# When VectorE makes its sums: gates moved to the turning of tokens, and the second layer's sums of weights made in two parts, in a mixture-of-experts kernel on one Trainium2 core

## The chip, the cores and the metric

The kernel runs on one core of a Trainium2 chip. Its time is the device time of one execution in microseconds (us); less is better. The engines appear in the profile under short names: PE is TensorE (matrix products; PEld is its loading of weights), DVE is VectorE, ACT is ScalarE, POOL is GpSimd, and SP is SyncE, whose queue issues most DMAs. Each engine works through its own queue in order and waits at an instruction until the semaphores that it names have been raised. A "bank" is one of the accumulators in PSUM that TensorE writes and the other engines read.

## What is computed

For 4096 tokens of 256 numbers, in float32:

```python
# graph layer
f = layernorm(x)
h = adj @ (f @ neigh_W.T) / (adj.sum(1) + 1)
x = x + concat([f, h]) @ lin_W.T
# attention (4 heads, 2 kv heads, causal), then a mixture of experts, on layernorm(x)
z = layernorm(x)
z = z + attention(rmsnorm(z)) @ wo.T
flat = rmsnorm(z)
weights = top 2 of softmax(flat @ router_w.T), made to add up to 1      # 8 experts
out = 0
for e in range(8):
    hh = silu(flat @ w1[e].T) * (flat @ w3[e].T)                        # 682 wide
    out = out + weights[:, e] * (hh @ w2[e].T)
x = x + z + out
```

The change touches the last loop alone. The number `weights[:, e]` of a token is called its gate here.

## The kernel before

The program has three stages: the graph layer to about 530 us, attention to about 1044 us, and the experts from there to the end. Tokens are not multiplied with all 8 experts. During attention each block of tokens is routed, and the row of a token (its 256 numbers, its number, its 8 gates) is scattered by GpSimd into the lists of its two experts in DRAM. The expert stage then works on groups: whole groups of 256 rows of one expert, and smaller ones of 128 rows for the ends of the lists. There are 42 turns, k = 0 to 41; `TURNS[k]` is the group of a turn. From k=9 whole and small groups alternate, with two small ones in a row at times.

Nothing is reordered by a scheduler: the order of each engine's queue is the order in which the functions below are called. The main loop calls, for each turn k: `hidden(k)` or `hidden_seven(k)` (first layer), then `combine(k - 1)` (second layer of the turn before, and scattering into the result), and then, if the group of turn k-1 was a whole one, `sums13` for a later turn. Loads of rows and weights are issued by SP four to five turns ahead.

What each function puts into the queues:

- `prepare(k)` (L1373) turns the rows of turn k on TensorE (L1379, tile `tx`) and ScalarE copies them, scaled, to SBUF (L1385, `xT`). For some turns it also makes sums of them on VectorE (`sums_x`, L1439). It is called for turn k+1 inside the first layer of turn k.
- `hidden(k)` multiplies in the plain way: products into banks `h` (L1656), ScalarE's silu (L1662), VectorE's multiply into `hT` (L1663, L1675). It takes six banks of the pool `e_h` in rotation, two at a time.
- `hidden_seven(k)` (L1445) does the first layer of a whole group with seven products in place of eight (a Strassen-Winograd scheme). It is used in 13 turns: k = 12, 14, 17, 19, 21, 23, 26, 28, 30, 33, 35, 37 and 39. The 682 columns are split into a part `one` of four chunks and a part `two` of one chunk; each has three banks, A, D and B, of the same six. Bank A takes several products one after another, and between them it has to be read: ScalarE copies it (L1490), VectorE adds it to a tile in SBUF (L1493). The tiles are `wqkv_sb` or `qT_all` (sums with banks B and D) and `hy` for part `one`, `hz` for part `two`. Four steps matter in what follows: `added_up` adds banks B and D, `third` adds bank A into `hy` or `hz`, `last` puts one more product into bank A, which must wait for that, and `multiplied` (L1521 to L1525) makes the hidden numbers, its second multiply (L1523) being the last reader of bank A. The first products of the next turn go into bank A of part `one`.
- `split(k)` (L1560) makes four sums of the hidden numbers on VectorE (L1571 to L1574), and `sums2(k)` four sums of the second layer's weights, called T1, T3, T2 and T4 in that order (L1589 to L1592), each 128x384. Both are inputs of `seven_products(k)` (L1595), the second layer of a whole group, which runs one turn later. In the 13 turns `hidden_seven` calls `sums2` before its first products; in the other turns with `seven_products` (k = 4 to 8 and 10) `split` calls it.
- `sums13` (L1410) makes four sums of a later turn's first-layer weights on GpSimd (L1422 to L1425), each 128x640.
- `combine(k)` (L1684) first computes the gates: VectorE multiplies the 8 gates of each row with a one-hot row of the group's expert (`pick`, L1691) and adds them up (`gt`, L1695). Then come the products of the second layer (L1613, or L1717 for small groups) into banks `ye_y` and `ye_ms`, seven VectorE adds for a whole group (L1621 to L1627), the multiplication with the gate (L1728 on ScalarE, L1734 on VectorE) and one or two scatters by GpSimd (L1739), which add the rows into DRAM. A scatter waits until that of the group before has landed.

The order of VectorE's work in `hidden_seven` is set by its last lines, of which these matter:

```python
            sums2(k)
            begun(one)
            second(one)
            added_up(one)
            step()
            begun(two)
            third(one)
            second(two)
            ...
            added_up(two)
            gated(one)
            third(two)
            step()
            if behind is not None:
                prepare(behind, p_ms, "ms")
            ...
            last(one)
            last(two)
            multiplied(one)
```

Of the kernel before, what the change touches and what calls it, by code (L numbers as in the profile page):

```python
# [9 lines left out]
F32 = mybir.dt.float32  # L10
# [3 lines left out]
ALU = mybir.AluOpType  # L14
AX = mybir.AxisListType
PSUM = bass.MemoryType.PSUM

P = 128
N = 4096
C = 256  # L20
# [4 lines left out]
NE = 8  # L25
# [36 lines left out]
ROW = C + 1 + NE  # L62
# [3 lines left out]
def fast_kernel(  # L66
# [24 lines left out]
    nc = tc.nc  # L91
# [89 lines left out]
    vv = [kvp.tile([P, TB, NKV * HD], F32, name=f"vv{b}") for b in range(NB)]  # L181
# [58 lines left out]
    with (  # L240
# [117 lines left out]
        G11, G12, G21, G22, T1, T2, T4 = range(7)  # L358
        T3 = G12
# [303 lines left out]
    with (  # L663
# [566 lines left out]
        mine = eg.tile([P, NG, NE], F32, name="mine")  # L1230
# [105 lines left out]
            at2 += (pt_all[:, at + 2 * W13 : at + 2 * W13 + W2],)  # L1336
        w13s = [a.rearrange("p (c w) -> p c w", c=2) for a in at13]
        w2s = [a.rearrange("p (k c) -> p k c", k=NF + 1) for a in at2]
        rows, hidden_of, inputs_of, expert_of = {}, {}, {}, {}


        def halves(i):
# [30 lines left out]
        def prepare(k, pool=p_y, tag="y"):  # L1373
            i = TURNS[k]
            n = halves(i)
            tr = pool.tile([P, 2, n, P], F32, tag=tag, name=f"tx_{i}")
            for h in range(n):
                for c in range(2):
                    nc.tensor.transpose(  # L1379
                        tr[:, c, h, :], rows[i][:, h, c * P : (c + 1) * P], ident  # L1380
                    )
            xT = late[:, LATE_XT + k % 2 * 2 * GR : LATE_XT + k % 2 * 2 * GR + 2 * n * P]
            xT = xT.rearrange("p (c i) -> p c i", c=2)
            for c in range(2):
                nc.scalar.activation(  # L1385
                    xT[:, c, :], tr[:, c].rearrange("p h i -> p (h i)"), AF.Copy,
                    scale=ln2_sb[:, c : c + 1],
                )
            inputs_of[i] = xT
            if k in SPLIT13:  # L1390
                sums_x(k, tr)

# [4 lines left out]
        parts_of, sums13_of = {}, {}  # L1399
# [28 lines left out]
        def sums_x(k, tr):  # L1428

            xT = inputs_of[TURNS[k]]  # L1430
            room = kT[6 + SPLIT13.index(k) % 2].rearrange("p (n i) -> p n i", n=4)
            m = {f"T{n + 1}": room[:, n] for n in range(4)}
            for c in range(2):
                for h in range(2):
                    m[f"B{c + 1}{h + 1}"] = xT[:, c, h * P : (h + 1) * P]
            for dst, c, h, less in (
                ("T1", 0, 1, "B11"), ("T2", 1, 1, "T1"), ("T3", 1, 1, "B12"), ("T4", 1, 0, "T2"),
            ):
                nc.vector.scalar_tensor_tensor(  # L1439
                    m[dst], tr[:, c, h, :], ln2_sb[:, c : c + 1], m[less],  # L1440
                    op0=ALU.mult, op1=ALU.subtract,
                )
            sums13_of[k].update(m)

        def hidden_seven(k, step, behind):  # L1445

            i = TURNS[k]
            m, xT, w13_sb = sums13_of.pop(k), inputs_of.pop(i), w13s[k % 5]
# [58 lines left out]
            def added_up(q):  # L1507
                added(q.s1, q, q.B)
                added(q.u2, q, q.D)

            def third(q):
                product(q, q.A, "S3", "T3")
                added(q.s5, q, q.A)
# [7 lines left out]
            def multiplied(q):  # L1521
# [2 lines left out]
                    hT[:, q.rows, 0:P], q.s1, q.A[:, 0 : len(q.chunks), :]  # L1524
                )  # L1525

            sums2(k)
            begun(one)
            second(one)
            added_up(one)  # L1530
            step()
            begun(two)
            third(one)
# [7 lines left out]
            added_up(two)  # L1541
            gated(one)
            third(two)
            step()
            if behind is not None:
                prepare(behind, p_ms, "ms")
# [13 lines left out]
        def split(k, hT):  # L1560


            m = {}
            for c in range(2):
                chunks = hT.rearrange("p (j c) i -> p c j i", c=2)[:, c]
                for h in range(2):
                    m[f"A{h + 1}{c + 1}"] = chunks[:, :, h * P : (h + 1) * P]
            for n, s in enumerate(("S1", "S2", "S4")):
                m[s] = kT[k % 2 * 3 + n][:, 0 : 3 * P].rearrange("p (j i) -> p j i", j=3)
            m["S3"] = m["A21"]  # L1570
            nc.vector.tensor_add(m["S1"], m["A21"], m["A22"])  # L1571
            nc.vector.tensor_sub(m["S2"], m["S1"], m["A11"])
            nc.vector.tensor_sub(m["S4"], m["A12"], m["S2"])
            nc.vector.tensor_sub(m["S3"], m["A11"], m["A21"])  # L1574
            if k not in parts_of:
                sums2(k)
            parts_of[k].update(m)

        def sums2(k):

            m = {}
            for c in range(2):
                weights = w2s[k % 5].rearrange("p (j c) o -> p c j o", c=2)[:, c]
                for h in range(2):
                    m[f"G{c + 1}{h + 1}"] = weights[:, :, h * P : (h + 1) * P]
            for n, s in enumerate(("T1", "T2", "T4")):
                m[s] = vv[k % 2 * 3 + n][:, 0:3, :]
            m["T3"] = m["G12"]
            nc.vector.tensor_sub(m["T1"], m["G12"], m["G11"])  # L1589
            nc.vector.tensor_sub(m["T3"], m["G22"], m["G12"])  # L1590
            nc.vector.tensor_sub(m["T2"], m["G22"], m["T1"])
            nc.vector.tensor_sub(m["T4"], m["T2"], m["G21"])  # L1592
            parts_of[k] = m

        def seven_products(k):  # L1595

# [87 lines left out]
        def combine(k):  # L1684
            i = TURNS[k]
            n = halves(i)
            w2_sb = w2s[k % 5]
            hT = hidden_of.pop(i)
            r = rows.pop(i)
            pick = ex.tile([P, n, NE], F32, tag="pick", name=f"pick_{i}")  # L1690
            nc.vector.tensor_mul(  # L1691
                pick, r[:, 0:n, C + 1 : ROW], mine[:, i : i + 1, :].to_broadcast([P, n, NE])
            )
            gt = ex.tile([P, n, 1], F32, tag="gt", name=f"gt_{i}")
            nc.vector.tensor_reduce(gt, pick, AX.X, ALU.add)  # L1695
            if k < ALONE or k % 2:
                y = ax.tile([P, HALF, C], F32, tag="yT1", name=f"y_{i}")
            else:
                y = (
                    pt_all[:, 2 * (2 * W13 + W2) :] if k % 4  # L1700
                    else wo_sb.rearrange("p j o -> p (j o)")[:, 0:512]
                ).rearrange("p (h c) -> p h c", h=HALF)

            last = k >= NM - 2
            seven = k in SEVEN
            if seven:
                done = seven_products(k)
            else:
                ps = [
                    pool.tile([P, HALF, C], F32, tag=tag, name=f"ye_{i}_{tag}")  # L1710
                    for pool, tag in ((p_ms, "ms"), (p_y, "y"))[0 if last else 1 :]
                ]

            def products(h):
                cols = slice(h * P, (h + 1) * P)
                for q in range(NF + 1):
                    nc.tensor.matmul(  # L1717
                        ps[h if last else 0][:, h, :],
                        hT[:, q, cols], w2_sb[:, q, :], start=(q == 0), stop=(q == NF),
                    )  # L1720

            for h in range(0 if last or seven else n):
                products(h)
            for h in range(n):
                if last:
                    products(h)
                if seven or n == 1:
                    nc.scalar.activation(  # L1728
                        y[:, h, :],
                        done[h].rearrange("p h o -> p (h o)") if seven else ps[0][:, h, :],  # L1730
                        AF.Copy, scale=gt[:, h],
                    )
                else:
                    nc.vector.tensor_scalar(  # L1734
                        y[:, h, :], ps[h if last else 0][:, h, :], gt[:, h], None, op0=ALU.mult
                    )
                at = bass.IndirectOffsetOnAxis(ap=r[:, h, C : C + 1].bitcast(I32), axis=0)
                nc.gpsimd.memset(gap, 0.0)  # L1738
                put = nc.gpsimd.indirect_dma_start(  # L1739
                    out=(acc_dram if k < NM - LAST else out)[:, :],  # L1740
                    out_offset=at,
                    in_=y[:, h, :], in_offset=None, compute_op=ALU.add,
                )
                if h:
                    free(put, f"half {i}", "an expert has a token once")
                else:
                    join(put, f"half {i}")
                if i < NA:
                    free(put, "last x", "the tokens of the first groups are others")
                    join(put, "first sums")  # L1750
# [86 lines left out]
        def step():  # L1837
            for f in next(rest, []):
                f()
# [776 lines left out]
```

## Time and profile before

| | us |
|---|---|
| median of 3 runs | 1550.57 |
| lowest and highest run | 1549.93, 1553.36 |
| profiled execution | 1554.68 |
| its span, first to last instruction | 1552.9 |
| TensorE busy in the span | 1533.3 |
| TensorE busy, 1044 to 1535 us (491 us of the expert stage) | 487.6 |
| VectorE busy, 1044 to 1535 us | 322.9 |
| GpSimd busy, 1044 to 1535 us | 208.0 |

The profile is one execution, taken by the hardware profiler. Lines of a timeline give the start in us from the span's start, the duration, the engine, the line of the kernel, the operation, and "out<-in" by the names of tiles, with partitions times elements and the count; in brackets stands how long the engine was idle before it, and what ended that. Groups of one line give minimum, median and maximum in ns. A list of waits gives who waited for whom, with the total, the number of waits and the longest. TensorE's matrix products are pipelined and their ends are modelled: the row of one can overlap the next by some 0.2 us. The granted clock of TensorE is 0.998 over the span.

### The profile page before, as it was taken

What the parts mean: (1) busy time and instruction counts of PE and PEld (TensorE: products, weight loads), DVE (VectorE), ACT (ScalarE), POOL (GpSimd) and SP (SyncE); (2) the same over time, 40 slices, a digit from 0 to 9 for tenths busy, and PEclk for the clock granted to TensorE, in tenths of its full rate; (3) what the DMA queues carried; (4) which work ended last, traced back from release to release, by engine and by line L of the source; (5) the groups of instructions that cost most, each with busy time, mean ns of one, the idle gap of its engine ahead of it and who ended that gap; (6) DMA issues with size and microseconds to landing.
All of it is one profiled execution on the core that took longest, in us unless ns stands there. A gap on an engine that the chain in (4) does not pass through costs nothing. (4 is left out here: it accounts for less than half of the span.)

```text
span 1552.9 us, 28593 instructions
## 1 busy us (share of the span) xinstructions
PE 1533.3 (99%) x11082; PEld 1138.0 (73%) x11082; DVE 1124.1 (72%) x2263; ACT 517.5 (33%) x966; POOL 741.4 (48%) x777
## 2 busy tenths in 40 slices
PE   8999999999999999999999999999999999999997
PEld 7888888888888643444444444358899999999996
DVE  7966677766766677778879878785565667677772
ACT  1101010010010255555656555553122433333331
POOL 3446456565565423364564563442424545545342
PEclk9999999999999999999999999999999999999999
DMA  6434444443434100001010111048676778777855
GB/s 237 129 128 147 139 139 136 139 139 136 139 136 139 35 1 16 29 31 52 32 57 23 39 39 33 25 149 320 205 229 212 223 235 257 243 231 253 264 144 133
DMA packets 68513, 209.42 MB, mean 135 GB/s; under 512 B 17488, under 2 KB 45520, under 8 KB 54736
## 3 DMA queue, kind: packets, MB, share of 16 engines
q1 hardware_dynamic: 55104, 189.50, 35.5%
q0 software_dynamic: 12720, 17.47, 5.7%
q8 instruction: 89, 1.46, 0.4%
q10 hardware_dynamic: 544, 0.52, 0.1%
q14 instruction: 56, 0.46, 0.1%
HBM read 184.48 MB, written 27.13 MB: 136 GB/s over the span
## 5 line engine op out<-in xcount | busy, mean ns | idle before, releaser
L759 PE MATMUL sc<-qT_all,kT 64*64 64x512 f32 (+3 forms) x2304 | 282.0, 557 | 1.0 <-ACT pt_all L767 0.5
L493 PE MATMUL acc<-a,g 128*128 128x256 f32 x1024 | 245.9, 380 | 0.0
L493 PEld LDWEIGHTS acc<-a,g 128*128 128x128 f32 x1024 | 193.0, 190 | 31.5 <-DVE vv L511 1.2
L759 PEld LDWEIGHTS sc<-qT_all,kT 64*64 64x64 f32 x2304 | 91.2, 133 | 130.0 <-issue 108.2
L767 ACT ACTIVATE pt_all<-sc 128x1024 f32<-128x1024 f32 (+3 forms) x157 | 148.9, 955 | 95.8 <-PE sc L759 95.0
L448 POOL TENSOR_TENSOR all_s<-all_s,more_sums 128x512 f32<-128x512 f32 x72 | 105.9, 1483 | 106.8 <-DVE more_sums L440 106.8
L1739 POOL DMA_INDIRECT acc_dram<-y,late x40 | 63.1, 1577 | 179.0 <-ACT y L1728 60.3
L493 PE MATMUL acc<-more_sums,g 128*128 128x256 f32 x512 | 126.2, 379 | 0.0
L787 DVE TENSOR_TENSOR late<-late,pt_all 128x1024 f32<-128x1024 f32 (+3 forms) x92 | 107.6, 1170 | 23.3 <-ACT pt_all L767 9.2
L493 PEld LDWEIGHTS acc<-more_sums,g 128*128 128x128 f32 x512 | 97.2, 190 | 14.7
L1656 PE MATMUL h<-late,qT_all 128*128 128x256 f32 (+1 forms) x616 | 105.1, 327 | 0.6 <-DMA qT_all<-in_w_dram 0.6
L801 PE MATMUL y_second<-pt_all,vv 64*64 64x512 f32 (+3 forms) x440 | 105.0, 555 | 0.0
L801 PE MATMUL y_first<-pt_all,vv 64*64 64x512 f32 (+3 forms) x440 | 104.3, 553 | 0.0
L1663 DVE TENSOR_TENSOR late<-si,h 128x256 f32<-128x256 f32 (+2 forms) x87 | 39.6, 465 | 87.7 <-ACT si L1662 57.6
L1656 PEld LDWEIGHTS h<-late,qT_all 128*128 128x128 f32 x616 | 94.0, 191 | 10.2 <-ACT late L1385 1.4
L1037 POOL DMA_INDIRECT lists<-row,slots x64 | 88.3, 1380 | 18.0 <-issue 15.0
L801 PE MATMUL y_third<-pt_all,vv 64*64 64x512 f32 (+3 forms) x376 | 89.8, 557 | 0.0
L378 ACT COPY qT_all<-tr 128x512 f32<-128x512 f32 x30 | 16.2, 589 | 210.5 <-PE tr L376 210.4
L1662 ACT ACTIVATE si<-h 128x256 f32<-128x256 f32 (+2 forms) x87 | 36.0, 422 | 115.7 <-PE h L1656 115.7
L769 POOL TENSOR_SCALAR_AFFINE_SELECT pt_all<-pt_all 128x256 f32<-128x256 f32 x36 | 21.7, 605 | 107.8 <-ACT pt_all L767 80.1
L1656 PE MATMUL h<-late,pt_all 128*128 128x128 f32 (+1 forms) x440 | 65.7, 306 | 0.0
L493 PE MATMUL acc<-qT_all,g 128*128 128x256 f32 x256 | 65.7, 379 | 0.0
(482 smaller groups left out, 3533.6 us busy)
## 6 DMA issues: line engine op xcount, KB each, us to landing
a<-in_adj_dram SPq DMA_DIRECT2D x64, 1024.0 KB, 4.8
qT_all<-in_w_dram SPq DMA_DIRECT2D x18, 1408.0 KB, 9.0
pt_all<-in_w_dram SPq DMA_DIRECT2D x16, 1408.0 KB, 8.8
res_all<-in_w_dram SPq DMA_DIRECT2D x17, 768.0 KB, 5.3
pt_all<-in_w_dram SPq DMA_DIRECT2D x16, 768.0 KB, 5.0
res_all<-in_w_dram SPq DMA_DIRECT2D x8, 1408.0 KB, 8.1
qT_all<-in_w_dram SPq DMA_DIRECT2D x9, 768.0 KB, 4.8
late<-lists SPq DMA_DIRECT2D x25, 265.0 KB, 2.8
```

Source lines behind the costliest of these rows:

```text
L448: nc.gpsimd.tensor_add(all_s[:, i], all_s[:, i], sums_at[n % 2][k])
L493: nc.tensor.matmul(acc[bank][:, at, :], g[jb][:, right, k, :], m[left][:, k, :], start=(jb == 0 and k == 0 and at == 0), stop=(jb == NB - ...
L759: nc.tensor.matmul(ps[k * HP : (k + 1) * HP, j, :w], kT[sb][hd, i * P + k * HP : i * P + (k + 1) * HP], qT[b][hd, p, off:], start=True, st ...
L767: nc.scalar.activation(pt[:, :, :w], ps[:, :, :w], AF.Exp, scale=HD ** -0.5)
L769: nc.gpsimd.affine_select(out=pt[:, :, 0:P], in_=pt[:, :, 0:P], pattern=[[0, 2], [1, P]], compare_op=ALU.is_ge, fill=0.0, base=0, channel_ ...
L787: nc.vector.tensor_add(sums[b, p][:, :, off:], before[:, :, off:], pt[:, :, : 512 - off])
L801: nc.tensor.matmul(accs[b, p][k][hd, off:], vv[sb][some, i, hd], pt[some, j, : 512 - off], start=(s == order_of(b)[0]), stop=(s == order_o ...
L1037: put = nc.gpsimd.indirect_dma_start(out=lists[:, :], out_offset=bass.IndirectOffsetOnAxis(ap=chosen[b][:, k, t, :], axis=0), in_=flats[b] ...
L1656: nc.tensor.matmul(ps[m % 2][:, m // 2 - q, :], w13_sb[:, c, m * P : (m + 1) * P], xT[:, c, :], start=(c == 0), stop=(c == 1),)
L1662: nc.scalar.activation(si[:, 0:both, :], ps[0][:, 0:both, :], AF.Silu)
L1663: nc.vector.tensor_mul(hT[:, q : q + both, :], si[:, 0:both, :], ps[1][:, 0:both, :])
L1739: put = nc.gpsimd.indirect_dma_start(out=(acc_dram if k < NM - LAST else out)[:, :], out_offset=at, in_=y[:, h, :], in_offset=None, comput ...
```

## The change

Two things move in VectorE's queue; no other engine's queue is different, and no instruction is added or removed.

First, the gates of turn k are computed in `prepare(k)`, after the tokens are turned and their sums made, and no longer at the start of `combine(k)`. They are kept in three buffers.

Second, `sums2` takes a list of the sums to make. In `hidden_seven` it isn't called before the first products any more: T1 and T3 are made after `added_up(one)`, T2 and T4 after `third(two)`, ahead of `prepare` of the next turn and of `multiplied`. `split` makes all four at once, in the order of before.

```diff
@@ prepare
             if k in SPLIT13:
                 sums_x(k, tr)
+            pick = ex.tile([P, n, NE], F32, tag="pick", name=f"pick_{i}")
+            nc.vector.tensor_mul(
+                pick, rows[i][:, 0:n, C + 1 : ROW],
+                mine[:, i : i + 1, :].to_broadcast([P, n, NE]),
+            )
+            gates_of[i] = ex.tile([P, n, 1], F32, tag="gt", name=f"gt_{i}", bufs=3)
+            nc.vector.tensor_reduce(gates_of[i], pick, AX.X, ALU.add)
@@ hidden_seven
-            sums2(k)
             begun(one)
             second(one)
             added_up(one)
+            sums2(k, ("T1", "T3"))
             step()
             begun(two)
             third(one)
@@
             added_up(two)
             gated(one)
             third(two)
+            sums2(k, ("T2", "T4"))
             step()
             if behind is not None:
                 prepare(behind, p_ms, "ms")
@@ split
             if k not in parts_of:
-                sums2(k)
+                sums2(k, ("T1", "T3", "T2", "T4"))
@@ sums2
-            nc.vector.tensor_sub(m["T1"], m["G12"], m["G11"])
-            nc.vector.tensor_sub(m["T3"], m["G22"], m["G12"])
-            nc.vector.tensor_sub(m["T2"], m["G22"], m["T1"])
-            nc.vector.tensor_sub(m["T4"], m["T2"], m["G21"])
-            parts_of[k] = m
+            m = parts_of[k]
+            for s in which:
+                a, b = {
+                    "T1": ("G12", "G11"), "T3": ("G22", "G12"),
+                    "T2": ("G22", "T1"), "T4": ("T2", "G21"),
+                }[s]
+                nc.vector.tensor_sub(m[s], m[a], m[b])
@@ combine
-            pick = ex.tile([P, n, NE], F32, tag="pick", name=f"pick_{i}")
-            nc.vector.tensor_mul(
-                pick, r[:, 0:n, C + 1 : ROW], mine[:, i : i + 1, :].to_broadcast([P, n, NE])
-            )
-            gt = ex.tile([P, n, 1], F32, tag="gt", name=f"gt_{i}")
-            nc.vector.tensor_reduce(gt, pick, AX.X, ALU.add)
+            gt = gates_of.pop(i)
```

More of the change, by code (lines that the diff above doesn't have):

```diff
@@ L1338, in fast_kernel @@
         w2s = [a.rearrange("p (k c) -> p k c", k=NF + 1) for a in at2]
-        rows, hidden_of, inputs_of, expert_of = {}, {}, {}, {}
+        rows, hidden_of, inputs_of, expert_of, gates_of = {}, {}, {}, {}, {}
         def halves(i):
@@ L1575, in split, with sums2 @@
             if k not in parts_of:
-                sums2(k)
+                sums2(k, ("T1", "T3", "T2", "T4"))
             parts_of[k].update(m)
[L1579 to L1592, printed above, removed]
-            parts_of[k] = m
+        def sums2(k, which):
+            if k not in parts_of:
+                m = parts_of[k] = {}
+                for c in range(2):
+                    weights = w2s[k % 5].rearrange("p (j c) o -> p c j o", c=2)[:, c]
+                    for h in range(2):
+                        m[f"G{c + 1}{h + 1}"] = weights[:, :, h * P : (h + 1) * P]
+                for n, s in enumerate(("T1", "T2", "T4")):
+                    m[s] = vv[k % 2 * 3 + n][:, 0:3, :]
+                m["T3"] = m["G12"]
+            m = parts_of[k]
[5 more added lines that the diff above has]
+                nc.vector.tensor_sub(m[s], m[a], m[b])
         def seven_products(k):
```

## The prediction

> **What bounds the kernel now.** I read the page first, for the engine that has no slack:
>
> ```profile
> PE 1533.3 (99%) x11082; PEld 1138.0 (73%) x11082; DVE 1124.1 (72%) x2263; ACT 517.5 (33%) x966; POOL 741.4 (48%) x777
> ```
>
> TensorE sets the end. VectorE counts only where TensorE waits for it, so next come TensorE's waits in the expert stage, 1040 us to the end (total, times, longest):
>
> ```profile
> PE hA L1484 <- DVE hy L1493: 1.7, 2, 0.9
> PE ye_y L1613 <- ACT y L1728: 1.5, 1, 1.5
> PE h L1656 <- DMA qT_all<-in_w_dram: 0.6, 1, 0.6
> ```
>
> So VectorE can be blamed for 3.2 us, in three places. The timeline around the first wait (turn k=26) shows why; VectorE, then GpSimd:
>
> ```profile
> 1356.02 1.88 DVE L1589 TENSOR_TENSOR vv<-res_all 128x384 f32<-128x384 f32 x1
> 1357.94 1.78 DVE L1590 TENSOR_TENSOR res_all<-res_all 128x384 f32<-128x384 f32 x1
> 1359.64 1.89 DVE L1591 TENSOR_TENSOR vv<-res_all,vv 128x384 f32<-128x384 f32 x1
> 1361.56 0.56 DVE L1592 TENSOR_TENSOR vv<-vv,res_all 128x384 f32<-128x384 f32 x1
> ...
> 1363.36 0.68 DVE L1493 TENSOR_TENSOR hy<-hy,hA 128x512 f32<-128x512 f32 x1
> ```
>
> ```profile
> 1355.95 1.54 POOL L1423 TENSOR_TENSOR res_all<-res_all,pt_all 128x640 f32<-128x640 f32 x1
> 1357.57 1.74 POOL L1424 TENSOR_TENSOR res_all<-pt_all,res_all 128x640 f32<-128x640 f32 x1
> 1359.27 1.85 POOL L1425 TENSOR_TENSOR pt_all<-pt_all 128x640 f32<-128x640 f32 x1
> ```
>
> The four sums of `sums2` take 0.56 us alone (fourth row) and 1.78 to 1.89 while GpSimd makes the four sums of `sums13`: the engines take turns. A VectorE operation with two SBUF operands that meets a GpSimd sum ends 0.42 us after that sum (1357.49 to 1357.90), and the next GpSimd sum ends 1.40 after VectorE's. Adds that read a bank do not take part: all L1493 rows of 128x512 lie between 678 and 689 ns, several inside GpSimd sums. So a sum beside GpSimd costs 1.8 instead of 0.56, and what matters is who queues behind it.
>
> The second place, 1438 us, looks the same. In the third (1394.7), the tile's `pick` stands behind sums of `split` so delayed, ScalarE's y waits for the gate, and `seven_products` for its bank.
>
> Then I read a usual turn, k=12 (VectorE, GpSimd, TensorE):
>
> ```profile
> 1215.15 0.69 DVE L1493 TENSOR_TENSOR wqkv_sb<-wqkv_sb,hD 128x512 f32<-128x512 f32 x1 [0.68 <-PE hD L1484]
> 1216.64 0.69 DVE L1493 TENSOR_TENSOR hy<-hy,hA 128x512 f32<-128x512 f32 x1 [0.81 <-PE hA L1484]
> ...
> 1218.62 0.68 DVE L1522 TENSOR_TENSOR late<-wqkv_sb,hy 128x512 f32<-128x512 f32 x1
> 1219.41 0.69 DVE L1523 TENSOR_TENSOR late<-wqkv_sb,hA 128x512 f32<-128x512 f32 x1
> ```
>
> ```profile
> 1214.95 2.12 POOL L1422 TENSOR_TENSOR res_all<-pt_all 128x640 f32<-128x640 f32 x1
> 1217.16 1.55 POOL L1423 TENSOR_TENSOR res_all<-res_all,pt_all 128x640 f32<-128x640 f32 x1
> ```
>
> ```profile
> 1218.19 1.28 PE L1484 MATMUL hA<-kT,res_all 128*128 128x128 f32 x10
> 1219.31 2.76 PE L1717 MATMUL ye_y<-res_all,late 128*128 128x256 f32 x12
> 1221.90 1.95 PE L1656 MATMUL h<-late,pt_all 128*128 128x128 f32 x16
> ```
>
> `sums2` is over (1213.87) before GpSimd begins (1214.95). VectorE owes TensorE two things: the hy add (ends 1217.33) before `last(one)` at 1218.19, slack 0.86; and `multiplied(one)`, whose L1523 empties bank A (ends 1220.10) before the next turn's h at 1221.90, slack 1.80.
>
> **The change, part by part.** In the built programs only VectorE's order differs; the other four queues keep theirs, SP's loads and POOL's scatters included, and no instruction is added or lost.
>
> *Gates.* `pick` and `gt`, 0.16 each and 0.38 with gaps, leave `combine`, which ends the 1.5 us wait. They now stand in `prepare`: in `hidden` among or behind its multiplies, where VectorE idles (L1663 waits 57.6 us in all on ScalarE, 30.1 on TensorE), so I take 0; if that cover fails in all 28 such turns it is 28 x 0.38 = 11 us, and beyond the 1.5 no wait on a gate is left to be saved. In `hidden_seven` they stand before `multiplied`.
>
> *T1, T3 after the first two bank adds.* In k=26 and 33 hB and hD are then added on time, GpSimd is done before the sums begin, and the 1.7 us of waits go. In k=12, VectorE is free at 1215.84, inside L1422, which ends 1217.08. T1 ends at 1217.50, L1423 at 1218.90, T3 at 1219.32, hy at about 1219.99: `last(one)` starts near 1220.04, not 1218.19. **Stall 1.85.**
>
> *T2, T4 and the gate before `multiplied`.* The same turn: hz adds to 1220.60, L1424 to 1220.72, T2 to 1221.14, L1425 to 1222.54, T4 to 1222.96, gate to 1223.35, L1522 and L1523 to 1224.80. The next h, now due at 1221.90 + 1.85 = 1223.75, waits 1.05. **Together 2.9 us.**
>
> Where L1422 starts late (k=30: 1408.05 against L1522 at 1409.40), T1 and T3 run free: hy is 0.33 later, inside its 0.86. But T2 waits for L1422 (to 1410.59), T4 for L1423 (12.41), pick for L1424 (13.84), L1522 for L1425 (15.96); L1523 ends at 1416.75, and h was due at 1412.68: **4.1 us**. With L1422 at 1387.11, 0.96 after L1522 (k=28), pick and L1522 are caught: 1392.25 against 1389.21, **3.0 us**.
>
> Where GpSimd is elsewhere (k=17, 26, 33, 39) the order costs 0.33 before hy and 2 x 0.57 + 0.38 = 1.5 before L1523, inside 0.86 and 1.80. That cover is thin: 0.3 is left.
>
> L1422's place in the 13 turns, by its start against L1522: 3.1 to 3.7 ahead in four (k=12, 14, 21, 23), 1.2 to 1.4 ahead in four (19, 30, 35, 37), behind in one. Sum as they stand: 4 x 2.9 + 4 x 4.1 + 3.0 = 31.0. GpSimd's start hangs on its own scatters, each waiting for the one before to land; k=30 and 37 follow a turn that the stalls lengthen, so their scatter should no longer be late and they join the first group: 6 x 2.9 + 2 x 4.1 + 3.0 = 28.6. Less the 3.2: **+25.4 us**. The profiled execution (1554.7, span 1552.9) would become 1580; it is 4.1 above the median of the runs, 1550.6, which becomes **1576**.
>
> What no row shows is the price of the lock at the new places: at least nothing (an operation slips between two GpSimd sums), at most 2.11, the longest that `pick` waited (1429.35). I take 1.8, the three rows of the same operations.
>
> The Trainium skill, "SBUF — State Buffer", section "Who interferes with whom", says that a VectorE instruction with two SBUF inputs and a GpSimd one that reads SBUF exclude each other, and the second to issue blocks until the first has finished. The rows agree on who blocks, but show only 0.42 of 0.56 us left afterwards; with the full length after each block the sum would rise by about 0.14 x 4 x 9 = 5 us.
>
> **Rivals.**
> 1. *Not slower: the bank adds were the point, and the sums fit in the gaps.* TensorE waits only on hy and bank A. If T1 and T3 fit in the 0.81 us gap and T2, T4 in 1.80, the 3.2 us go and nothing returns: 1547. For it: the slacks hold without GpSimd. Against: L1422 starts 0.9 us before T1 would in k=12. It decides if GpSimd's sums start over 4 us after L1522.
> 2. *Only one of the two dues is missed.* GpSimd shifts, or TensorE's bank order leaves more room than 1.80: with the 1.85 in six turns alone, 11 - 3 = +8, 1559.
> 3. *More is late.* All nine turns cost 4.1, or late `split` sums hold up `seven_products` too: 37 and more, 1588 upward.
>
> **Chances.** Forecast (+15 to +37): 0.66, own range 1566 to 1588. Rival 2 (+3 to +15): 0.14. Rival 1: 0.14, of which 0.09 faster by over 0.2% (3.1 us, about what a measurement of this kernel can tell from no change) and 0.05 within it. Rival 3: 0.06. Slower by over 0.2%: 0.66 + 0.14 + 0.06 = 0.86. The range takes the forecast and rival 2, 1554 to 1588, 0.80.
>
> **What would show it.** New waits of `hA` (last products) on VectorE's hy, about 1.8 each in some six turns; new waits of `h` on VectorE's bank-A multiply, 1 to 4 in nine; T1, T2, T4 or pick at 1.4 to 2.1 us beside L1422 to L1425 (seven lines lower after the change); no wait of `ye_y` on ScalarE. TensorE's busy time stays and the span grows, all between 1200 and 1490 us. Wrong if those sums stay at 0.56, or if GpSimd's sums begin after `multiplied`.

## The result and the profile after

| | before | after | ratio, 95% interval |
|---|---|---|---|
| median, us | 1551.8 (6 runs) | 1564.62 (6 runs) | 1.0085, 1.0072 to 1.0098 |
| profiled execution, us | 1554.68 | 1565.87 | |
| its span, us | 1552.9 | 1564.2 | |

The change makes the kernel slower by 12.8 us. Forecast were 25.4 us: the sign is right, the size is half. The measured 1564.6 lies just below the forecast's own range (1566 to 1588) and in that of rival 2, by which only one of the two dues is missed. The page's first line of the changed kernel:

```profile
PE 1535.0 (98%) x11082; PEld 1138.7 (73%) x11082; DVE 1122.5 (72%) x2263; ACT 523.7 (33%) x966; POOL 740.1 (47%) x777
```

TensorE's and VectorE's busy times moved by under 2 us, while the span grew by 11.3: it is waiting that was added. TensorE's waits from 1040 us to the end (total, times, longest) are now one line; the old three are gone:

```profile
PE hA L1491 <- DVE hy L1500: 14.2, 9, 1.6
```

Nine waits, all in the nine turns whose GpSimd sums fall into `hidden_seven`. The list counts from the modelled end of a matrix product; from start to start each is 1.73 to 1.75 us, 15.7 in all. (Lines are seven lower than before the change: L1500 is the add from a bank, L1491 the products, L1429 to L1432 GpSimd's sums, L1604 all sums of `sums2`.) The turn k=12, first VectorE:

```profile
1214.38 0.69 DVE L1500 TENSOR_TENSOR wqkv_sb<-wqkv_sb,hD 128x512 f32<-128x512 f32 x1 [1.10 <-PE hD L1491]
1214.98 1.70 DVE L1604 TENSOR_TENSOR vv<-res_all 128x384 f32<-128x384 f32 x1
1216.72 1.78 DVE L1604 TENSOR_TENSOR res_all<-res_all 128x384 f32<-128x384 f32 x1
1218.42 0.68 DVE L1500 TENSOR_TENSOR hy<-hy,hA 128x512 f32<-128x512 f32 x1
...
1219.61 0.71 DVE L1604 TENSOR_TENSOR vv<-res_all,vv 128x384 f32<-128x384 f32 x1
1220.36 1.78 DVE L1604 TENSOR_TENSOR vv<-vv,res_all 128x384 f32<-128x384 f32 x1
...
1223.11 0.69 DVE L1530 TENSOR_TENSOR late<-wqkv_sb,hA 128x512 f32<-128x512 f32 x1
```

GpSimd in the same stretch:

```profile
1214.12 2.13 POOL L1429 TENSOR_TENSOR res_all<-pt_all 128x640 f32<-128x640 f32 x1
1216.34 1.75 POOL L1430 TENSOR_TENSOR res_all<-res_all,pt_all 128x640 f32<-128x640 f32 x1
1218.16 1.74 POOL L1431 TENSOR_TENSOR res_all<-pt_all,res_all 128x640 f32<-128x640 f32 x1
1219.87 1.85 POOL L1432 TENSOR_TENSOR pt_all<-pt_all 128x640 f32<-128x640 f32 x1
```

And TensorE:

```profile
1217.20 0.38 PE L1379 MATMUL tx<-ident,late 128*128 128x128 f32 x2
1219.16 1.38 PE L1491 MATMUL hA<-kT,res_all 128*128 128x128 f32 x10 [1.57 <-DVE hy L1500]
1220.37 2.76 PE L1723 MATMUL ye_y<-res_all,late 128*128 128x256 f32 x12
1222.97 1.95 PE L1667 MATMUL h<-late,pt_all 128*128 128x128 f32 x16
1224.75 0.60 PE L1379 MATMUL tx<-ident,late 128*128 128x128 f32 x4
1225.19 2.06 PE L1667 MATMUL h<-late,pt_all 128*128 128x128 f32 x17
```

Read them against each other. T1 waits for L1429 (ends 1216.25) and ends 0.43 after it, T3 for L1430 (ends 1218.09) and ends 0.41 after it; hy follows, and the product into bank A starts 0.06 after hy, at 1219.16 in place of 1217.42. What the prediction expected next does not happen: h at 1222.97 follows the products before it without a gap, though VectorE empties bank A of part `one` only at 1223.80.

### The profile page after: what moved, and what is told of

Same layout as the page of the kernel before. It is cut to its first block, busy times and chain, and to the rows that moved or that the text cites. A ratio compares the mean times of both kernels' runs of the same rounds, so it can differ in the third digit from the quotient of the medians.

```text
span 1564.2 us, 28567 instructions
## 1 busy us (share of the span) xinstructions
PE 1535.0 (98%) x11082; PEld 1138.7 (73%) x11082; DVE 1122.5 (72%) x2263; ACT 523.7 (33%) x966; POOL 740.1 (47%) x777
## 5 line engine op out<-in xcount | busy, mean ns | idle before, releaser
L787 DVE TENSOR_TENSOR late<-late,pt_all 128x1024 f32<-128x1024 f32 (+3 forms) x92 | 107.8, 1171 | 23.4 <-ACT pt_all L767 9.4
```

The source lines that it names most:

```text
L787: nc.vector.tensor_add(sums[b, p][:, :, off:], before[:, :, off:], pt[:, :, : 512 - off])
```

## The experiments

Theory L: the loss is T1 and T3, each held up by a GpSimd sum, in front of the hy add. Rivals: P, two sums in that place are too much whatever GpSimd does; G, the earlier gates are part of the loss. Every kernel was timed beside before (median 1552.6 of 29 runs for the first four kernels, 1552.6 of 19 for the rest).

| kernel | median, us | ratio to before, 95% interval | TensorE's waits in the expert stage, by lines of the list |
|---|---|---|---|
| gates alone | 1548.24 | 0.9977, 0.9966 to 0.9988 | hy: 1 |
| sums alone | 1568.27 | 1.0105, 1.0082 to 1.0127 | hy: 7, y: 2, others: 2 |
| without GpSimd's sums | 1548.47 | 0.9976, 0.9965 to 0.9987 | none |
| by turn | 1548.30 | 0.9978, 0.9968 to 0.9987 | none |
| one sum | 1553.91 | 1.0024, 1.0012 to 1.0035 | h on `multiplied`: 1 |
| all late | 1557.74 | 1.0047, 1.0032 to 1.0062 | h on `multiplied`: 9 |
| sums in split | 1550.31 | 0.9984, 0.9971 to 0.9998 | second layer: 4 |

**Gates alone.** `hidden_seven` makes the four sums at its start again.

```diff
+            sums2(k, ("T1", "T3", "T2", "T4"))
             begun(one)
             second(one)
             added_up(one)
-            sums2(k, ("T1", "T3"))
...
             third(two)
-            sums2(k, ("T2", "T4"))
```

> The gates move to prepare as in the changed kernel, but hidden_seven makes all four sums of sums2 at its start, as before. Theory L (the loss is T1 and T3, each held up by a GpSimd sum, in front of the hy add): the nine waits of about 1.74 us are gone, the 1.6 us wait on ScalarE's y is gone too, the two waits on hy in k=26 and 33 stay at up to 1.1 us each; 1.5 to 2.5 us below before, about 1549. Theory G (earlier gates are part of the loss: they free scatters sooner, or pick delays VectorE): slower than before by several us.

Measured 4.3 us below before by the medians. The list of TensorE's waits has one line left:

```profile
PE hA L1491 <- DVE hy L1500: 1.1, 1, 1.1
```

It is the turn k=33; the wait of k=26 is gone too, which wasn't expected, and so is that on y. The early gates are a gain. Theory G falls.

Early gates alone do not make the scatters of whole groups punctual, though. In six of the nine turns (k=19, 21, 28, 30, 35 and 37) the first scatter starts 1.1 to 3.2 us after the first half of its y is ready, as here in k=28 (ScalarE makes both halves of y, 0.5 us each; then GpSimd's first scatter):

```profile
1376.96 1.03 ACT L1733 ACTIVATE pt_all<-vv,gt 128x256 f32<-128x256 f32 x2 [2.39 <-DVE vv L1635]
1380.70 1.56 POOL L1744 DMA_INDIRECT acc_dram<-pt_all,late  x1 [8.96 <-ACT qT_all L1497]
```

**Sums alone.** The changed `hidden_seven`, with the gates in `combine` as before.

```diff
@@ prepare
-            nc.vector.tensor_mul(
-                pick, rows[i][:, 0:n, C + 1 : ROW],
-                mine[:, i : i + 1, :].to_broadcast([P, n, NE]),
-            )
-            nc.vector.tensor_reduce(gates_of[i], pick, AX.X, ALU.add)
@@ combine
-            gt = gates_of.pop(i)
+            nc.vector.tensor_mul(
+                pick, rows[i][:, 0:n, C + 1 : ROW],
+                mine[:, i : i + 1, :].to_broadcast([P, n, NE]),
+            )
+            nc.vector.tensor_reduce(gt, pick, AX.X, ALU.add)
```

> sums2 in two parts as in the changed kernel, gates in combine as before. Theory L: a stall of 1.74 us in each turn whose GpSimd sums begin before T1; with gates late the scatters of small groups are late as well, so in some of the nine turns GpSimd starts after T3 and the stall is less: 4 to 9 stalls, 5 to 14 us above before. Theory P (two sums in that place are too much whatever GpSimd does): thirteen stalls. Theory G: near before, under 4 us above.

It is the slowest of all, 15.7 us above before, and above the 5 to 14 expected. The waits of TensorE on hy and y:

```profile
PE hA L1484 <- DVE hy L1493: 13.0, 7, 2.9
PE ye_y L1617 <- ACT y L1732: 1.7, 1, 1.7
PE ye_y L1617 <- ACT pt_all L1732: 1.6, 1, 1.6
```

Five of the seven waits on hy are 1.73 to 1.76 from start to start, two are longer (2.4 in k=21, 3.1 in k=35): there T1 came while GpSimd was still at the scatter ahead of its sums, was held until the end of the first sum, and took 2.36 and 3.07. In k=19 and k=28 there is none: their scatters started 2.6 and 2.8 us after the first half of y was ready, so GpSimd's sums came after T3. (A scatter waits for the one before to land. In k=21 and 35 that landing is on record, and the scatter starts 0.72 us after it; in k=19 and 28 it isn't.) In those two turns a later wait of 1.8 us on y, through a late gate, takes its place. The nine waits come to about 17.8 us. With the gates early, in the changed kernel, every whole group's first scatter starts 0.28 us after the first half of its y. So the gates do not make the loss, but they help to decide where GpSimd's sums stand, and both parts together cost less than the sums alone.

**Without GpSimd's sums.** The changed kernel; the four sums of `sums13` are left out, and the products work with what lies in those rooms.

```diff
@@ sums13
-            nc.gpsimd.tensor_add(m["S1"], m["A21"], m["A22"])
-            nc.gpsimd.tensor_sub(m["S2"], m["S1"], m["A11"])
-            nc.gpsimd.tensor_sub(m["S4"], m["A12"], m["S2"])
-            nc.gpsimd.tensor_sub(m["S3"], m["A11"], m["A21"])
```

> The changed kernel without the four GpSimd sums of sums13: the weights' sums of the first layer are left out, the products go on with what lies there. Theory L: T1, T3, T2, T4 take 0.56 us each, no wait of hA on hy above 0.1 us; about 1548, 3 to 4 us below before. Theory P: the nine waits of 1.74 us stay, about 1564.

No wait is left. VectorE's timeline in k=12:

```profile
1214.84 0.55 DVE L1600 TENSOR_TENSOR vv<-res_all 128x384 f32<-128x384 f32 x1
1215.43 0.56 DVE L1600 TENSOR_TENSOR res_all<-res_all 128x384 f32<-128x384 f32 x1
1215.90 0.68 DVE L1496 TENSOR_TENSOR hy<-hy,hA 128x512 f32<-128x512 f32 x1
```

T1 and T3 stand in the same place with the same work and take 0.55 and 0.56, not 1.70 and 1.78; hy starts 1.06 after T1, not 3.44. Theory P falls.

**By turn.** The two parts only where GpSimd's sums meet the start of `hidden_seven`, after two small groups in a row (k=17, 26, 33); elsewhere all four sums at the start.

```diff
+            two_small = k - 2 not in SEVEN
+            if not two_small:
+                sums2(k, ("T1", "T3", "T2", "T4"))
             begun(one)
             second(one)
             added_up(one)
-            sums2(k, ("T1", "T3"))
+            if two_small:
+                sums2(k, ("T1", "T3"))
...
             third(two)
-            sums2(k, ("T2", "T4"))
+            if two_small:
+                sums2(k, ("T2", "T4"))
```

> The changed kernel, but sums2 stands in two parts only in turns that follow two small groups (k=17, 26, 33), where GpSimd's sums meet the start of hidden_seven; in the other ten all four sums stand at its start. Theory L: no wait of hA on hy at all and none of ye_y on y; 3 to 4.5 us below before, about 1547.5. Theory G: above 1550. If GpSimd's sums begin earlier than before with the earlier gates, and meet the sums at the start, new waits of hA on hy in some of the ten turns, up to 1 us each.

TensorE waits for nothing after the first turn. The busy times of PE, PEld, DVE, ACT and POOL (counts in brackets), the clock, the DMA share and GB/s from 1044 to 1530 us, first of this kernel, then of the changed one:

```profile
1044.00:1530.00 486.00, 486.00 (x3503) 460.96 (x3502) 309.75 (x788) 165.68 (x401) 206.67 (x205) 1.00 0.75 237
```

```profile
1044.00:1530.00 486.00, 471.80 (x3408) 446.12 (x3407) 317.05 (x774) 163.28 (x394) 204.61 (x201) 1.00 0.73 232
```

In 486 us TensorE is busy for 486.00 here and for 471.80 there: the 14.2 us of the list. VectorE in the turn k=26, the one of the prediction's first timeline:

```profile
1359.16 0.69 DVE L1500 TENSOR_TENSOR wqkv_sb<-wqkv_sb,hD 128x512 f32<-128x512 f32 x1 [1.10 <-PE hD L1491]
1359.76 0.55 DVE L1609 TENSOR_TENSOR vv<-res_all 128x384 f32<-128x384 f32 x1
1360.35 0.56 DVE L1609 TENSOR_TENSOR res_all<-res_all 128x384 f32<-128x384 f32 x1
1360.82 0.68 DVE L1500 TENSOR_TENSOR hy<-hy,hA 128x512 f32<-128x512 f32 x1
```

The two-part order does there what it can do, since GpSimd has finished by then (its fourth sum ends at 1357.85). By turn beats both kernels of the study; from the gates alone it cannot be told apart by time (0.9978 and 0.9977), only by the wait that it saves.

**One sum.** T1 alone stays in front of hy.

```diff
-            sums2(k, ("T1", "T3"))
+            sums2(k, ("T1",))
...
-            sums2(k, ("T2", "T4"))
+            sums2(k, ("T3", "T2", "T4"))
```

> The changed kernel with T1 alone after added_up(one); T3, T2, T4 after third(two). Theory L by its rows: T1 ends 0.42 us after the first GpSimd sum, hy follows at once and ends about when last(one) is due, so each wait of hA on hy falls from 1.74 to under 0.2 us; a third sum ahead of multiplied costs only if bank A is due early. About 1548 to 1551. Theory P (any work in that place shifts hy by its own length): 0.3 us each.

No wait on hy is left in the list: with one held-up sum the slack of 0.86 just suffices, with two it falls short by 1.74. But the time is 3 us above what was expected. TensorE's weight loads show where it went:

```profile
PEld ye_y L1624 <- DVE late L1582: 2.2, 9, 0.2
PEld h L1667 <- DVE late L1530: 1.1, 4, 0.4
```

Three sums ahead of `multiplied` make it late for bank A in four turns (0.2 to 0.4 us), and make `split` (L1582 is its last sum) late for `seven_products` in nine (0.22 each). Set product against product with by turn, where TensorE never waits, the nine turns lose 2.0 us at bank A (five of them under 0.2 each, which the list leaves out) and 2.9 behind `split`; the spans differ by 5.1.

**All late.** None of the sums before hy, all four ahead of `multiplied`.

```diff
-            sums2(k, ("T1", "T3"))
...
-            sums2(k, ("T2", "T4"))
+            sums2(k, ("T1", "T3", "T2", "T4"))
```

> The changed kernel with none of the four sums before hy; all four after third(two), ahead of multiplied. No wait of hA on hy. It tests when bank A of part one is due again. If the next turn's first product takes it (as the prediction had it): L1523 would end near 1225.3 in the time of before's k=12 turn, h was due at 1221.9, 3.4 us in each of nine turns, some 25 to 30 us above before. If only its fourth bank does (due near 1224.6): under 1 us each, 0 to 5 us above before, waits of h on VectorE at the second pair of banks.

Measured 5.2 us above before: about the second branch (0 to 5), far from the first (25 to 30). The waits of TensorE's products and of its weight loads, and TensorE in k=12:

```profile
PE h L1666 <- DVE late L1530: 4.5, 9, 0.6
```

```profile
PEld ye_y L1623 <- DVE late L1581: 2.2, 9, 0.3
```

```profile
1221.01 1.95 PE L1666 MATMUL h<-late,pt_all 128*128 128x128 f32 x16
1222.79 0.60 PE L1379 MATMUL tx<-ident,late 128*128 128x128 f32 x4
1223.23 0.61 PE L1666 MATMUL h<-late,pt_all 128*128 128x128 f32 x4
1224.27 2.94 PE L1666 MATMUL h<-late,pt_all 128*128 128x128 f32 x24 [0.43 <-DVE late L1530]
```

The sixteen products of the first two banks and the first four of the third run unhindered from 1221.01; TensorE stops at the fourth bank, 0.55 to 0.81 us from start to start in each of nine turns. L1530 ends at 1224.22, and the fourth bank's products start at 1224.27. So bank A is due 2.7 us later than the prediction had it (1223.23 + 0.45 against 1221.01). The second list is `split`, late for `seven_products` as in one sum.

**Sums in split.** `hidden_seven` makes none of the four sums; `split` makes them behind its own.

```diff
-            sums2(k, ("T1", "T3"))
...
-            sums2(k, ("T2", "T4"))
```

> The changed kernel without sums2 in hidden_seven: split makes all four behind its own sums, where before and after the turns of the first kind do it too. No wait on hy; multiplied as early as before. The sums end 2.3 us later than split did, up to 4 us where GpSimd still runs; seven_products of the turn comes 3 us after split's end in k=12 and 1 us after it in k=30. Theory L: 0 to 0.5 us of waits of ye_y on VectorE's sums in a few turns; 1548 to 1550.

About 2 us below before. GpSimd's sums now meet `split`, and where VectorE is late by that the second layer waits; TensorE's waits:

```profile
PE ye_ms L1622 <- DVE pick L1393: 1.6, 3, 0.7
PE ye_y L1622 <- DVE late L1580: 1.3, 1, 1.3
```

One wait of 1.4 us, start to start, is longer than the 0.5 expected. It is in k=28, where GpSimd's sums delay three sums of `split` to 1.20, 1.78 and 1.78 us, so that the last (L1580) ends at 1394.58. The place is better than that of the change. Against that of before (gates alone, 2.1 us less by the medians) the intervals overlap, so no difference is shown.

## Why the prediction was right in sign and twice too large

- **The 3.2 us of old waits go: right.** No wait on y is left in the changed kernel, and by turn, which also has none on hy, is 4.3 us below before by the medians.
- **T1 and T3 held up in front of hy, 1.85 us a turn: right in mechanism and size**, 1.74 measured in each of nine turns. The working for k=12 has T1 end 0.42 us after GpSimd's first sum and T3 1.82 after T1; measured 0.43 and 1.82 (1216.68 to 1218.50). Without GpSimd's sums the same order costs nothing.
- **T2, T4 and gate ahead of `multiplied`, another 1.05 us: wrong.** The sums are held up as worked out (T4 1.78 us), and bank A of part `one` is emptied late, at 1223.80. The step that failed is "The next h, now due at 1221.90 + 1.85 = 1223.75, waits 1.05", and with it the sentence ahead of the prediction that the first products of the next turn go into that bank. In the built program they do not: banks are handed out in the order in which they were released, so after each of the 13 turns the next one takes bank B of part `one`, bank D of part `one`, bank D of part `two`, and bank A of part `one` only as the fourth. All late measured when it is due. The prediction read an order of banks from the order of the calls, and the slack of 1.80 that it took from there was never the real one, which is 4.5 (1.80 + 2.7). So what came is rival 2 in its second form, "TensorE's bank order leaves more room than 1.80", to which the prediction gave 0.14; it has the stall in nine turns, where rival 2 reckoned with six.
- **Turns whose scatters are late, 4.1 and 3.0 us: none is left.** The prediction moved two of five such turns to the first group, because the stalls lengthen the turns before. All five moved: in the changed kernel each of the nine groups is scattered 0.28 us after the first half of its y. In the one profile of each kernel it takes both halves of the change. With the stalls but late gates (sums alone) four of the nine are still 0.9 to 2.8 us after y; with early gates but no stalls (gates alone) six are, by 1.1 to 3.2. A pair of a whole and a small turn lasts 21.5 us in gates alone and 23.4 in the changed kernel, and in the two kernels between, one sum and all late (22.0 and 22.5), no group is late either. So these kernels agree with the prediction's reason; that the early gates are needed with it was not in the prediction, which had them as work to be placed and as the end of the wait on y.
- **Gates in `prepare` at no cost: right.** No wait of TensorE on them appears in the changed kernel, gates alone or by turn, and the gates alone are a gain of 0.23%.

Summed anew with the runs: 9 x 1.74 = 15.7, less the 3.7 that before's three waits come to from start to start, is 12.0; measured 12.8 by the medians, 11.2 by the two profiled executions. The forecast had 28.6 us of new waits, 12.9 more than the 15.7: 6 x 1.05 = 6.3 is bank A, 6.0 are the three odd turns (11.2 forecast, 3 x 1.74 = 5.2 measured), the rest 6 x 0.11 from the stall itself.

Left open: before's runs spread from 1548 to 1556 us, those of the gates alone from 1547 to 1552. That late scatters come and go from run to run would explain it: gates alone and by turn are 0.1 us apart by the medians, but their one profile each has six and three late groups among the nine. With one profiled execution of each kernel this is not shown.

## What to carry to other kernels

An engine with a quarter of its time free can still cost time: ask what each of its operations would take beside another engine that it has to take turns with, and keep operations that can be held up out of the place between a bank's product and the add that frees it. Move work off the front of such an add only into a stretch where the other engine is known to be idle, turn by turn if the turns differ. And before a slack is read off a bank, read from the built program which bank each product gets; the order of the calls doesn't tell it.

## What the runs showed of the hardware

- VectorE's additions with both operands in SBUF and GpSimd's sums take turns. A 128x384 addition took 0.55 to 0.56 us alone; one that met a GpSimd sum with more than 0.1 us of it left ended 0.41 to 0.43 after the end of that sum, in every kernel and every place that it was put. Where both queues were full the two alternated, and the addition took 1.70 to 1.90; GpSimd's later sums, 1.54 alone, then took 1.73 to 2.01. Without GpSimd's sums nearly all additions were at 0.55 to 0.56, none above 0.60.
- Additions that read a bank were not touched (128x512: 0.67 to 0.69 beside GpSimd's sums in every kernel), nor was the reduction of the gates (0.16 to 0.17).
- What an addition pays is what is left of the other engine's operation when it comes to the front of its queue: in the changed kernel's k=12, T2 began 0.29 us before the end of GpSimd's third sum and took 0.71 in place of 1.78. With sums alone, k=35, T1 began 0.52 before the row of GpSimd's first sum, during the scatter ahead of it, and took 3.07.
